# A cross-attention block on Trainium2: another order for the first units, V for two groups of heads at once, and x loaded ahead of the second K chain's weights

## The chip, the cores and the metric

The kernel runs on one core of one Trainium2 chip. The metric is the device time of one execution in microseconds. The core has five engines that run side by side, each through its own list of instructions in program order, and wait for one another by semaphores: TensorE (PE in the profile) multiplies matrices, VectorE (DVE) and ScalarE (ACT) do elementwise work, GpSimd (POOL) does small elementwise work, and SyncE (SP) issues most of the transfers (DMAs). Products land in PSUM and are copied ("evacuated") to SBUF by DVE or ACT.

## What is computed

One transformer block with cross-attention, in float32, for B = 4 batches of 512 tokens of width 512, 16 heads of 32, and an inner width of 2048. The mask, here all ones, is applied too.

```python
x = layer_norm(hidden_states, ln1_w, ln1_b)
q = (x @ q_w + q_b).reshape(B, LQ, H, HD).transpose(0, 2, 1, 3)
k = (encoder_hidden_states @ k_w + k_b).reshape(B, LK, H, HD).transpose(0, 2, 1, 3)
v = (encoder_hidden_states @ v_w + v_b).reshape(B, LK, H, HD).transpose(0, 2, 1, 3)
scores = jnp.einsum('bhqd,bhkd->bhqk', q, k) * scale
scores = jnp.where(mask, scores, mask_value)
out = jnp.einsum('bhqk,bhkd->bhqd', jax.nn.softmax(scores, axis=-1), v)
hidden = out.transpose(0, 2, 1, 3).reshape(B, LQ, D) @ cproj_w + cproj_b + residual
y = layer_norm(hidden, ln2_w, ln2_b)
y = jax.nn.gelu(y @ fc_w + fc_b, approximate=True) @ proj_w + proj_b
return hidden + y
```

## The kernel before

The attention is cut into 16 units w = 0 to 15: four batches, and in each four groups of four heads (128 columns). Unit w belongs to batch w // 4. For each unit three "chains" of products are made: K (`prep_k`, line 235), Q (`prep_q`, line 245) and V (`prep_v`, line 257). K and Q have 512 moving columns and four blocks of the contraction; V computes 128 tokens by 128 columns at a time, four token tiles by four blocks. In the trace each float32 product shows as two passes, so a K chain is 8 matmuls and a V chain 32. ACT evacuates every chain; POOL then adds V's bias (`v_bias`).

A unit has four quarters of 128 query tokens. A quarter is: `scores` (line 279: four products into the single PSUM tile sc; then DVE adds the mask and takes the least value, line 284, and ACT takes the exponential, line 288) and `turn` (line 302: DVE transposes blocks of 32 by 32 into a tile tb). After every second quarter the reciprocal of the sums is made on DVE (line 307), spread by ACT (line 309) and transposed (line 311), and `copies` (line 345) issues 16 DMAs on SP that exchange tb's blocks between partitions, into pT or a part of gt or xe. `attend` (line 362, "av") multiplies the result by V; it comes some quarters later, at places that the table `AT` sets.

The rest of PE's work is laid between the scores by hand: the lists `first[w]` and `later[w]`. Where `first[w]` is a tuple, its parts run after quarter 0, 1, 2 and 3 of the unit. `A(w)` is a unit's K, Q and V chain; `inputs(b)` is batch b's load of x, its first layer norm (three parts), the four transposed tiles "tp" (`ln1_turn`, line 176) and the load of the context (`load_enc`, into eT, which is the first half of xe). A chain's function also issues the next load into the weights that it has just used: K's, Q's and V's weights have two buffers each, and a load waits until the chain that used the buffer two units before is done. The context has one buffer, so batch 1's context may be loaded only when the last K and V chain of batch 0 are done; it is issued by the item that holds V3.

All these transfers go through SP, in program order: a DMA that waits holds back what is behind it, and what is issued runs on one queue. The first layer norm of batch b is normalised on DVE, and two of its four transposed tiles are evacuated there, unless (1, b) is in `BY_ACT`; then ACT does both. The transposed tiles, chains, av and output projections share four PSUM buffers, taken in turn (pool ps_acc).

The middle of the kernel adds the output projection (line 403), the second layer norm and the MLP (lines 469 and 479) between the scores; from about 560 us on the MLPs of the last batches run alone (lines 573 and 613).

Of the kernel before, what the change touches and what calls it, by code (L numbers as in the profile page):

```python
# [45 lines left out]
P = 128  # L46
# [17 lines left out]
IN_XE = (25, 27, 29, 31)  # L64

AT = {u: (u - 5) // 2 for u in (5, 7, 9, 11, 13, 15, 17, 19, 53, 55, 57, 59, 61, 63)}
BY_ACT = ((1, 1),)
MW = 8
WARM = 9
PW = 2 * NT * HG * HD  # L70
# [7 lines left out]
def xattn_block(ctx: ExitStack, tc: tile.TileContext, x, encT, mask, q_w, k_w, v_w, c_w, fc_w, p_w, vecs, rows, out):  # L78
# [3 lines left out]
    def pools(stack, **bufs):  # L82
        return [stack.enter_context(tc.tile_pool(name=n, bufs=k)) for n, k in bufs.items()]

    const, keep, hids, tiles, small = pools(ctx, const=1, keep=1, hids=6, tiles=4, small=4)
    dram = ctx.enter_context(tc.tile_pool(name="dram", bufs=1, space=bass.MemoryType.DRAM))
    ps_acc = ctx.enter_context(tc.tile_pool(name="ps_acc", bufs=4, space=PSUM))

    att = ctx.enter_context(ExitStack())
    one, two, five = pools(att, one=1, two=2, five=5)  # L90
    ps_sc = att.enter_context(tc.tile_pool(name="ps_sc", bufs=1, space=PSUM))
    ctx.enter_context(tc.manual_schedule())

# [34 lines left out]

    def kqv_w(w, i):
        n = 4 * i + 2 + w % 2  # L130
        return ptt[:, n * D : (n + 1) * D].rearrange("p (d f) -> p d f", d=ND)

    S = {}
# [6 lines left out]

    def ln_stat(key, t, src):
        if t == 0:
            S["mv", key] = small.tile([P, NT, 2], F32, tag="mv", name=f"mv{key[0]}_{key[1]}")
        st = small.tile([P, 6], F32, tag="st", name=f"st{key[0]}_{key[1]}_{t}")
        nc.vector.bn_stats(st, src)
        nc.vector.bn_aggr(S["mv", key][:, t, :], st)

    def ln_rs(key):

        ve = small.tile([P, NT], F32, tag="ve", name=f"ve{key[0]}_{key[1]}")  # L150
        nc.gpsimd.tensor_scalar(ve, S["mv", key][:, :, 1], EPS, 1.0, ALU.add, ALU.mult)
        rs = small.tile([P, NT], F32, tag="rs", name=f"rs{key[0]}_{key[1]}")
        nc.gpsimd.tensor_tensor(rs, ve, nhalf, ALU.pow)
        S["rs", key] = rs
        if key in BY_ACT:
            nm = small.tile([P, NT], F32, tag="nm", name=f"nm{key[0]}_{key[1]}")
            nc.gpsimd.tensor_tensor(nm, S["mv", key][:, :, 0], rs, ALU.mult)
            nc.gpsimd.tensor_scalar(nm, nm, -1.0, 0.0, ALU.mult, ALU.add)
            S["nm", key] = nm
# [60 lines left out]
    def load_w(w, queue=None, names=("wk", "wq", "wv")):  # L220

        if w >= NW:
            return
        g = w % NG
        for i, (n, src) in enumerate((("wk", k_w), ("wq", q_w), ("wv", v_w))):
            if n in names:
                S[n, w] = kqv_w(w, i)
                (queue or Q[0]).dma_start(out=S[n, w], in_=src[:, g, :, :])

    def prep_k(w):  # L230
        b, g = divmod(w, NG)
        kT = k_q(w, 0)
        acc = acc_tile(f"acck_{w}")
        for d in range(ND):
            nc.tensor.matmul(acc, S["wk", w][:, d, :], eT[:, d, :], start=(d == 0), stop=(d == ND - 1))  # L235
        load_w(w + 2, names=("wk",))
        nc.scalar.activation(kT, acc, AF.Identity, bias=vec[:, KB + g : KB + g + 1], scale=1.0)
        S["kT", w] = kT
# [10 lines left out]
        S["qT", w] = qT  # L249

    def prep_v(w):
        b = w // NG
        v = five.tile([P, NT, P], F32, tag="v", name=f"v_{w}")
        acc = acc_tile(f"accv_{w}")
        for t in range(NT):
            for d in range(ND):
                nc.tensor.matmul(  # L257
                    acc[:, ts(t, P)], eT[:, d, ts(t, P)], S["wv", w][:, d, :],
                    start=(d == 0), stop=(d == ND - 1),
                )  # L260
        load_w(w + 2, names=("wv",))
        nc.scalar.copy(v, acc.rearrange("p (t f) -> p t f", t=NT))  # L262
        S["v", w] = v
        if w:
            v_bias(w)

    def v_bias(w):
        v, bias = S["v", w], row[:, 2, ts(w % NG, P)]
        nc.gpsimd.tensor_tensor(v, v, bias[:, None, :].broadcast_to([P, NT, P]), ALU.add)  # L269


    def scores(w, qt):
        if qt == 0:
            S["sums", w] = small.tile([P, NT, HG], F32, tag="sums", name=f"sums_{w}")
        qT, kT, sums = S["qT", w], S["kT", w], S["sums", w]
        sc = ps_sc.tile([P, HG, L], F32, tag="sc", name=f"sc_{w}_{qt}")
        for h in range(HG):
            r = slice(h * HD, (h + 1) * HD)
            nc.tensor.matmul(sc[:, h, :], qT[r, ts(qt, P)], kT[r, :], start=True, stop=True)  # L279
        ps = []  # L280
        for h in range(HG):
            s = score_tile()
            mn = small.tile([P, 1], F32, tag="mn", name=f"mn_{w}_{qt}_{h}")
            nc.vector.tensor_tensor_reduce(  # L284
                out=s, in0=sc[:, h, :], in1=S["mb", w // NG], scale=1.0, scalar=FMAX,
                op0=ALU.add, op1=ALU.min, accum_out=mn,
            )
            nc.scalar.activation(s, s, AF.Exp, bias=mn, scale=-1.0, accum_out=sums[:, qt, h : h + 1])  # L288
            ps.append(s)
        S["ps", w, qt] = ps  # L290

    def turn(w, qt):

        half, q = divmod(qt, 2)
        if q == 0:


            S["tb", w, half] = two.tile([P, NI, PW + 2 * HD], F32, tag="tb", name=f"tb_{w}_{half}")
        tb = S["tb", w, half]
        tv = tb[:, :, :PW].rearrange("p j (a t h q) -> p a h t j q", a=2, t=NT, h=HG)  # L300
        for h in range(HG - q):
            nc.vector.transpose(tv[:, q, h], S["ps", w, qt][h])  # L302
        if q == 0:
            return

        rs = small.tile([P, 2, HG], F32, tag="rsum", name=f"rsum_{w}_{half}")
        nc.vector.reciprocal(rs, S["sums", w][:, 2 * half : 2 * half + 2, :])
        rr = one.tile([P, 2, HG, HD], F32, tag="rr", name=f"rr_{w}_{half}")
        nc.scalar.copy(rr, rs[:, :, :, None].broadcast_to([P, 2, HG, HD]))
        nc.vector.transpose(tv[:, q, HG - 1], S["ps", w, qt][HG - 1])  # L310
        nc.vector.transpose(
            tb[:, :, PW:].rearrange("p j (a q) -> p a j q", a=2), rr.rearrange("p a h d -> p (a h d)")
        )
        waiting.append((w, half))
        if w < NW - 1 or half == 0:
            exchange()
# [31 lines left out]
    def attend(w, half):  # L348

        b, g = divmod(w, NG)  # L350
        if g == 0 and half == 0:
            S["oT", b] = one.tile([P, NG, L], F32, tag="oT", name=f"oT_{b}")
        v, pT = S["v", w], S["pT", w, half]
        av = acc_tile(f"av_{w}_{half}")
        o = S["oT", b][:, g, ts(half, 2 * P)]
        shape, kw = "p (a i q) -> p a i q", dict(a=2, i=NI)
        pv = pT[:, :, :PW].rearrange("p i (a t h q) -> p t h a i q", a=2, t=NT, h=HG)
        p = [[pv[:, t, h] for h in range(HG)] for t in range(NT)]
        r = pT[:, :, PW:].rearrange("p i (a q) -> p a i q", a=2)
        for t in range(NT):  # L360
            for h in range(HG):
                nc.tensor.matmul(  # L362
                    av[ts(h, HD), : 2 * P].rearrange(shape, **kw), v[:, t, ts(h, HD)], p[t][h],
                    start=(t == 0), stop=(t == NT - 1),
                )
        o, a = o.rearrange(shape, **kw), av[:, : 2 * P].rearrange(shape, **kw)
        nc.vector.tensor_tensor(o, a, r, ALU.mult)
        if (w, half) in held:
            held.remove((w, half))
        exchange()  # L370
# [386 lines left out]
    make_identity(nc, ident)  # L757
    nc.gpsimd.memset(nhalf, -0.5)
    load_enc(0)
    load_w(0, nc.sync, ("wv",))  # L760
    load_x(0)
    load_w(1, nc.sync, ("wk",))
    load_w(0, nc.sync, ("wq",))

    warm = acc_tile("warm")
    for _ in range(WARM):
# [7 lines left out]
    for part in range(3):  # L774
        ln1(0, part)
    prep_k(0)
    prep_v(0)
    prep_k(1)
    run(turns1(0))
    x1, x2, x3, x4 = inputs(1)  # L780
    run(x1)
# [13 lines left out]
    k5, q5, v5 = A(5)  # L795
    k6, q6, v6 = A(6)
    first[0] = (
        [(CHAIN, lambda: prep_v(1))], [(CHAIN, lambda: prep_q(1)), k2] + x2[:1], [k3, v2] + x2[1:2],
        [(CHAIN, lambda: (prep_v(3), load_enc(1)))]
    )  # L800
    first[1] = [q2] + x2[2:], [q3], [k4], x3[:2]
    first[2] = x3[2:] + [v4], [q4], [k5], [v5]
    first[3] = [q5], [k6], [q6], [v6] + do(lambda: c_bias(0))
    mlp = []
    for p in range(SPLIT):
        mlp += FC(p, 0) + FC(p, 1) + PJ(p, 0) + FC(p, 2) + PJ(p, 1) + FC(p, 3) + PJ(p, 2) + PJ(p, 3)
# [24 lines left out]
    def norm(b, *ts_):  # L831
# [7 lines left out]
    later[4] = c[:1] + x2[:1] + c[1:2] + x2[1:2] + c[2:3] + x2[2:] + c[3:]  # L839
    k, q, v = A(8)  # L840
    first[5] = (
        [k] + stat(0, 0, 1, 2, 3) + rs(0) + x3 + norm(0, 0, 1, 2, 3), [v, q] + t2, some(2) + pb_(0), some(2)
    )
    k, q, v = A(9)
    x1, x2, x3, x4 = inputs(3)
# [2 lines left out]
    first[7] = [k, q] + x2[:1] + some(2) + x2[1:2] + some(3) + [v]  # L848

    k, q, v = A(11)  # L850
    first[8] = h_(1, 0, 1) + x2[2:] + [k, q] + x3[:2] + some(1) + x3[2:] + [v] + h_(1, 2, 3) + x4
    later[8] = cb(1) + C(1)
    k, q, v = A(12)
    first[9] = [q] + some(2) + [k] + some(2) + [v]
# [110 lines left out]
```

## Time and profile before

| | us |
|---|---|
| median of 3 runs | 813.45 |
| lowest, highest | 812.35, 814.26 |
| the profiled execution | 812.55 |
| its span, first to last instruction | 810.8 |
| PE busy, in the span | 793.0 |
| DVE busy | 556.2 |
| ACT busy | 355.6 |
| POOL busy | 98.0 |

PE is the busiest engine by far. Some of its work around the place of the change, by PE's timeline: the passes of K0 begin at 5.35 us, V0's at 9.07, K1's at 12.64, the transposed tiles of x at 16.08, Q0's at 17.83, and the first scores at 22.20. The scores of unit 1 begin at 48.29, those of unit 2 at 77.10 and those of unit 3 at 101.85.

```profile
DVE  3786898986678765767778998736738993368511
...
PEclk9998999999999999999999999999999999999999
DMA  8888998857797867688668799883335330023001
```

These are lines of the page's 40 equal slices (20.3 us each): the tenths in which DVE was busy, the clock that the throttle granted to PE, and the share of the DMA engines' time. DVE and the transfers are near their full share in the first 140 us.

### The profile page before, as it was taken

To read this page: it belongs to the slowest core of one execution; us is meant where nothing else is said; L and a number is where in the kernel's file an instruction comes from. 1 tells how busy PE (TensorE), PEld (TensorE's weight loads), DVE (VectorE), ACT (ScalarE), POOL (GpSimd) and SP (SyncE) were. 2 spreads that over 40 slices of the span, in tenths; PEclk is the share of its full clock that TensorE was granted. 3 is DMA by queue.
4 is the path that set the end of the run, shared out by engine and by line. 5 is a ranking of instruction groups with operands and counts; after the bars stand their busy time and mean duration, and the time that the engine had idled before them with its cause. 6 is when DMAs were issued, how large, how long until landed. Compare 5 with 4: busy or idle time off the path is not lost.

```text
span 810.8 us, 11911 instructions
## 1 busy us (share of the span) xinstructions
PE 793.0 (98%) x4082; PEld 481.7 (59%) x4082; DVE 556.2 (69%) x1279; ACT 355.6 (44%) x779; POOL 98.0 (12%) x110
## 2 busy tenths in 40 slices
PE   9996999989999999999999999999999999999998
PEld 6453545454354554535554334445888888888887
DVE  3786898986678765767778998736738993368511
ACT  2664665358673646547644469700312330023200
POOL 1120003030000021001131000120050021200011
PEclk9998999999999999999999999999999999999999
DMA  8888998857797867688668799883335330023001
GB/s 327 284 206 222 210 240 240 236 141 187 187 247 169 230 171 214 164 209 204 158 150 218 189 270 234 208 247 128 97 111 175 112 116 14 27 79 91 1 14 39
DMA packets 60956, 137.14 MB, mean 169 GB/s; under 512 B 12464, under 2 KB 15664, under 8 KB 60768
## 3 DMA queue, kind: packets, MB, share of 16 engines
q1 hardware_dynamic: 59472, 132.43, 60.8%
q0 software_dynamic: 896, 2.82, 1.1%
q10 hardware_dynamic: 528, 1.14, 0.7%
q8 instruction: 32, 0.52, 0.3%
q14 instruction: 28, 0.23, 0.1%
HBM read 58.22 MB, written 6.82 MB: 80 GB/s over the span
## 4 chain that ended last, share of the span: by engine, by line
PE 86%; DVE 5%; SPq 5%; DMA 2%; issue 1%; ACT 0%; POOL 0%; DVEq 0%; POOLq 0%
PE q L573 15%; PE accf L469 9%; PE accp L479 8%; PE accc L403 7%; PE sc L279 7%; PE av L362 7%; PE acck L235 6%; PE accv L257 6%; PE accq L245 6%; SPq L345 5%; PE q5p L613 2%; PE q3p L613 2%; PE q7p L613 2%; PE q6p L613 2%; PE q1p L613 2%; PE q2p L613 2%
## 5 line engine op out<-in xcount | busy, mean ns | idle before, releaser
L288 ACT ACTIVATE ptt<-ptt,mn 128x512 f32<-128x512 f32 x256 | 181.6, 710 | 134.3 <-DVE mn L284 134.2
L284 DVE CUSTOM_DVE_ANT_0 ptt<-sc,mb 128x512 f32<-128x512 f32 x256 | 161.0, 684 | 46.0 <-PE sc L279 45.8
L302 DVE STREAM_TRANSPOSE tb<-ptt 128x512 f32<-128x512 f32 x224 | 142.0, 683 | 5.1 <-ACT ptt L288 5.1
L469 PE MATMUL accf<-yT,pbt 128*128 128x512 f32 x192 | 87.3, 601 | 0.0
L479 PE MATMUL accp<-pbt,gt 128*128 128x512 f32 x192 | 86.4, 600 | 0.0
L279 PE MATMUL sc<-pbt 32*128 32x512 f32 x512 | 73.0, 640 | 3.3 <-DVE mn L284 2.5
L573 PE MATMUL q<-ys,gt 128*128 128x256 f32 x320 | 75.1, 379 | 0.0
L235 PE MATMUL acck<-xe,ptt 128*128 128x512 f32 x128 | 62.0, 629 | 4.2 <-DMA xe<-encT_dram 4.2
L573 PEld LDWEIGHTS q<-ys,gt 128*128 128x128 f32 x320 | 60.8, 190 | 8.3
L257 PEld LDWEIGHTS accv<-ptt,xe 128*128 128x128 f32 x512 | 58.9, 192 | 10.8 <-issue 5.9
L469 PEld LDWEIGHTS accf<-yT,pbt 128*128 128x128 f32 x192 | 35.0, 190 | 50.2 <-issue 46.2
L479 PEld LDWEIGHTS accp<-pbt,gt 128*128 128x128 f32 x192 | 35.2, 190 | 48.6 <-issue 46.2
L257 PE MATMUL accv<-ptt,xe 128*128 128x128 f32 x512 | 60.7, 277 | 2.1 <-DVE xe L179 1.3
L573 PE MATMUL q<-yT,gt 128*128 128x256 f32 x240 | 58.1, 379 | 0.5 <-DVE gt L501 0.5
L245 PE MATMUL accq<-xe,ptt 128*128 128x512 f32 x128 | 58.3, 598 | 0.0
L403 PE MATMUL accc<-wc,oT 128*128 128x512 f32 x128 | 56.7, 597 | 0.0
L269 POOL TENSOR_TENSOR v<-v,row 128x512 f32<-128x512 f32 x16 | 20.5, 1281 | 286.1 <-ACT v L262 286.1
L577 ACT ACTIVATE ga<-uc,vec 128x256 f32<-128x256 f32 x40 | 20.3, 508 | 75.4 <-DVE uc L551 75.4
L573 PEld LDWEIGHTS q<-yT,gt 128*128 128x128 f32 x240 | 45.5, 190 | 7.4 <-DVE gt L501 0.9
L288 ACT ACTIVATION_READ_ACCUMULATOR ptt<-ptt,mn 128x1 f32 x256 | 47.8, 187 | 0.0
L235 PEld LDWEIGHTS acck<-xe,ptt 128*128 128x128 f32 x128 | 24.5, 200 | 39.2 <-issue 31.5
L362 PE MATMUL av<-pT,v 128*32 128x256 f32 x768 | 46.4, 382 | 0.8 <-DMA pT<-tb 0.8
(121 smaller groups left out, 917.4 us busy)
## 6 DMA issues: line engine op xcount, KB each, us to landing
pT<-tb SPq DMA_DIRECT2D x384, 136.0 KB, 2.4
pbt<-p_w_dram SPq DMA_DIRECT2D x40, 256.0 KB, 3.3
gt<-fc_w_dram SPq DMA_DIRECT2D x40, 256.0 KB, 2.7
gt<-tb SPq DMA_DIRECT2D x64, 136.0 KB, 2.5
xe<-tb SPq DMA_DIRECT2D x56, 136.0 KB, 3.1
pbt<-fc_w_dram SPq DMA_DIRECT2D x24, 256.0 KB, 4.3
ptt<-k_w_dram SPq DMA_DIRECT2D x16, 256.0 KB, 3.6
xe<-encT_dram SPq DMA_DIRECT2D x16, 256.0 KB, 4.5
```

Of the source, the lines that this page charges most:

```text
L235: nc.tensor.matmul(acc, S["wk", w][:, d, :], eT[:, d, :], start=(d == 0), stop=(d == ND - 1))
L245: nc.tensor.matmul(acc, S["wq", w][:, d, :], xT[:, d, :], start=(d == 0), stop=(d == ND - 1))
L257: nc.tensor.matmul(acc[:, ts(t, P)], eT[:, d, ts(t, P)], S["wv", w][:, d, :], start=(d == 0), stop=(d == ND - 1),)
L279: nc.tensor.matmul(sc[:, h, :], qT[r, ts(qt, P)], kT[r, :], start=True, stop=True)
L284: nc.vector.tensor_tensor_reduce(out=s, in0=sc[:, h, :], in1=S["mb", w // NG], scale=1.0, scalar=FMAX, op0=ALU.add, op1=ALU.min, accum_out=mn,
L288: nc.scalar.activation(s, s, AF.Exp, bias=mn, scale=-1.0, accum_out=sums[:, qt, h : h + 1])
L302: nc.vector.transpose(tv[:, q, h], S["ps", w, qt][h])
L362: nc.tensor.matmul(av[ts(h, HD), : 2 * P].rearrange(shape, **kw), v[:, t, ts(h, HD)], p[t][h], start=(t == 0), stop=(t == NT - 1),)
L403: nc.tensor.matmul(acc, S["oT", b][:, g, ts(t, P)], wc[:, g, :], start=(g == 0), stop=(g == NG - 1))
L469: nc.tensor.matmul(acc, S["fcw", b, f][:, d, :], S["yT", b][:, d, :], start=(d == 0), stop=(d == ND - 1))
L479: nc.tensor.matmul(acc, gT[q % 2][:, k, ts(t, P)], S["pw", b, q * FQ + k], start=(k == 0), stop=(k == FQ - 1))
L573: nc.tensor.matmul(o, a[:, k], y[:, k], start=(k == 0), stop=(k == 1))
```

## The change

V is computed for two groups of heads at once. `prep_v(w)` now makes half of the tokens for the 256 columns of units w and w + 1 (w even: token tiles 0 and 1; w odd: tiles 2 and 3), in products of 256 columns; the odd one completes V for both. The weights of a pair are one DMA of 512 KB into the place of the two old buffers, so there is one buffer, and the next pair's load is issued when the odd chain is done. V's tile holds two units, with three buffers instead of five.

At the start, x is loaded before the second K chain's weights, and V's weights after Q's; PE runs K0, K1, V0 instead of K0, V0, K1.

The order of the chains in units 0 to 3 is another. On PE, with sc 0_1 for the scores of unit 0, quarter 1, it was sc 0_0, V1, sc 0_1, Q1, K2, sc 0_2, K3, V2, sc 0_3, V3, sc 1_0, Q2, av, sc 1_1, Q3, sc 1_2, K4, av, sc 1_3, two tp tiles, sc 2_0, two tp tiles, V4, av, sc 2_1, Q4, sc 2_2, K5, av, sc 2_3, V5, sc 3_0. It becomes sc 0_0, V1, sc 0_1, V2, K2, sc 0_2, K3, V3, sc 0_3, Q1, sc 1_0, Q2, av, sc 1_1, K4, sc 1_2, V4, av, sc 1_3, Q3, sc 2_0, two tp tiles, K5, av, sc 2_1, two tp tiles, sc 2_2, V5, av, sc 2_3, Q4, sc 3_0. In unit 3, V6 and Q6 change places. The context's load for batch 1 stands one quarter earlier with V3, and so ahead of the second set of exchange copies on SP.

Batch 2's first layer norm goes to ACT. V8 stands before sc 5_1 instead of behind it, and V11 before the last tp tile of batch 3. Small statistics tiles have two buffers instead of four (pool few).

```diff
-BY_ACT = ((1, 1),)
+BY_ACT = ((1, 1), (1, 2))
...
     def kqv_w(w, i):
         n = 4 * i + 2 + w % 2
+        if i == 2:
+
+            return ptt[:, n * D : (n + 2) * D].rearrange("p (d f) -> p d f", d=ND)
         return ptt[:, n * D : (n + 1) * D].rearrange("p (d f) -> p d f", d=ND)
...
-            if n in names:
+            if n in names and (i < 2 or w % 2 == 0):
                 S[n, w] = kqv_w(w, i)
-                (queue or Q[0]).dma_start(out=S[n, w], in_=src[:, g, :, :])
+                (queue or Q[0]).dma_start(out=S[n, w], in_=src[:, g // 2 if i == 2 else g, :, :])
...
     def prep_v(w):
-        b = w // NG
-        v = five.tile([P, NT, P], F32, tag="v", name=f"v_{w}")
+
+        half, first = w % 2, w - w % 2
+        if half == 0:
+            S["v", first] = S["v", w + 1] = three.tile([P, NT, 2 * P], F32, tag="v", name=f"v_{w}")
+        v = S["v", w]
         acc = acc_tile(f"accv_{w}")
-        for t in range(NT):
+        for t in range(2):
             for d in range(ND):
                 nc.tensor.matmul(
-                    acc[:, ts(t, P)], eT[:, d, ts(t, P)], S["wv", w][:, d, :],
+                    acc[:, ts(t, 2 * P)], eT[:, d, ts(2 * half + t, P)], S["wv", first][:, d, :],
                     start=(d == 0), stop=(d == ND - 1),
                 )
-        load_w(w + 2, names=("wv",))
-        nc.scalar.copy(v, acc.rearrange("p (t f) -> p t f", t=NT))
-        S["v", w] = v
+        if half:
+            load_w(w + 1, names=("wv",))
+        nc.scalar.copy(v[:, ts(half, 2), :], acc.rearrange("p (t f) -> p t f", t=2))
...
-                    av[ts(h, HD), : 2 * P].rearrange(shape, **kw), v[:, t, ts(h, HD)], p[t][h],
+                    av[ts(h, HD), : 2 * P].rearrange(shape, **kw), v[:, t, ts(w % 2 * HG + h, HD)], p[t][h],
...
     load_enc(0)
-    load_w(0, nc.sync, ("wv",))
     load_x(0)
     load_w(1, nc.sync, ("wk",))
     load_w(0, nc.sync, ("wq",))
+    load_w(0, nc.sync, ("wv",))
...
     prep_k(0)
+    prep_k(1)
     prep_v(0)
-    prep_k(1)
     run(turns1(0))
...
     first[0] = (
-        [(CHAIN, lambda: prep_v(1))], [(CHAIN, lambda: prep_q(1)), k2] + x2[:1], [k3, v2] + x2[1:2],
-        [(CHAIN, lambda: (prep_v(3), load_enc(1)))]
+        [(CHAIN, lambda: prep_v(1))], [v2, k2] + x2[:1], [k3, (CHAIN, lambda: (prep_v(3), load_enc(1)))] + x2[1:2],
+        [(CHAIN, lambda: prep_q(1))]
     )
-    first[1] = [q2] + x2[2:], [q3], [k4], x3[:2]
-    first[2] = x3[2:] + [v4], [q4], [k5], [v5]
-    first[3] = [q5], [k6], [q6], [v6] + do(lambda: c_bias(0))
+    first[1] = [q2] + x2[2:], [k4], [v4], [q3]
+    first[2] = x3[:2] + [k5], x3[2:], [v5], [q4]
+    first[3] = [q5], [k6], [v6], [q6] + do(lambda: c_bias(0))
...
-        [k] + stat(0, 0, 1, 2, 3) + rs(0) + x3 + norm(0, 0, 1, 2, 3), [v, q] + t2, some(2) + pb_(0), some(2)
+        [k] + stat(0, 0, 1, 2, 3) + rs(0) + x3 + norm(0, 0, 1, 2, 3) + [v], [q] + t2, some(2) + pb_(0), some(2)
...
-    first[8] = h_(1, 0, 1) + x2[2:] + [k, q] + x3[:2] + some(1) + x3[2:] + [v] + h_(1, 2, 3) + x4
+    first[8] = h_(1, 0, 1) + x2[2:] + [k, q] + x3[:2] + some(1) + x3[2:3] + [v] + x3[3:] + h_(1, 2, 3) + x4
```

## The prediction

> **What bounds the kernel now.** The page first: TensorE (PE) is busy for 793.0 of 810.8 us, so what it loses in waits is nearly all there is to gain, and its waits come second.
>
> ```profile
> PE 793.0 (98%) x4082; PEld 481.7 (59%) x4082; DVE 556.2 (69%) x1279; ACT 355.6 (44%) x779; POOL 98.0 (12%) x110
> ```
>
> ```profile
> engine line waited for: us in total, times, longest us
> PE acck L235 <- DMA xe<-encT_dram: 4.2, 1, 4.2
> PE sc L279 <- DVE mn L284: 2.5, 2, 1.6
> PE tp L176 <- ACT v L262: 2.3, 1, 2.3
> ...
> PE accv L257 <- DVE xe L179: 1.3, 1, 1.3
> ```
>
> Third, PE's timeline over the place of the longest wait: K4, the first chain on batch 1's context, waits 4.25 us and then takes 6.57 us instead of 3.4.
>
> ```profile
> 59.56 1.14 PE L279 MATMUL sc<-pbt 32*128 32x512 f32 x8
> 64.95 6.57 PE L235 MATMUL acck<-xe,ptt 128*128 128x512 f32 x8 [4.25 <-DMA xe<-encT_dram]
> ...
> 77.10 1.14 PE L279 MATMUL sc<-pbt 32*128 32x512 f32 x8 [1.63 <-DVE mn L284]
> ```
>
> Fourth, why. The stage table (PEclk is the third number from the end) has the clock at half after the wait, from 63.98 (0.98 in the row of 63) to 70.78 (0.61 in that of 70); SP's queue shows the context's load behind sixteen exchange copies.
>
> ```profile
> 63.00:64.00 1.00, 0.00 (x0) 0.00 (x0) 1.00 (x5) 1.00 (x3) 0.00 (x0) 0.98 0.95 342
> 64.00:65.00 1.00, 0.05 (x1) 0.08 (x1) 1.00 (x3) 0.96 (x4) 0.00 (x0) 0.50 0.98 281
> ...
> 69.00:70.00 1.00, 1.00 (x2) 0.34 (x1) 0.00 (x0) 0.00 (x0) 0.00 (x0) 0.50 0.78 185
> 70.00:71.00 1.00, 1.00 (x3) 0.34 (x1) 0.00 (x0) 0.00 (x0) 0.00 (x0) 0.61 0.84 212
> 71.00:72.00 1.00, 1.00 (x14) 0.39 (x16) 0.00 (x0) 0.45 (x1) 0.00 (x0) 1.00 0.67 170
> ```
>
> ```profile
> 27.14 0.33 SPq L228 DMA_DIRECT2D ptt<-v_w_dram  x1
> 33.62 11.65 SPq L345 DMA_DIRECT2D pT<-tb  x16
> ...
> 50.03 10.36 SPq L345 DMA_DIRECT2D gt<-tb  x16
> 60.50 0.52 SPq L228 DMA_DIRECT2D ptt<-v_w_dram  x1
> 61.07 1.87 SPq L189 DMA_DIRECT2D xe<-encT_dram  x4
> ```
>
> Below, K4 is the K chain of unit 4, sc 1_2 the scores of unit 1, quarter 2. Steps are counted from start to start on PE's timeline: a chain inside a row of chains 3.43 us, between scores 3.63 (55.93 to 59.56), scores 1.07, av 1.87.
>
> **The change, part by part, with PE walked in its new order.**
>
> *V in 256 columns.* A V chain is 32 passes of 128 columns from 9.07 to 12.64, 3.57 us; afterwards 16 passes of 256. Line 613 runs sixteen such in a row from 585.16 to 588.62, 3.46 us. The saving is 0.12 us (rounded up) x 16 chains = 1.9 us; from below 0, if these operands run differently.
>
> *Context load.* V3 is done before sc 0_3, so the load of encT stands ahead of the second set of copies. By the walk V3 ends at 49.3 and the pieces land by 49.3 + 0.5 (V's own load) + 1.87 + 5.0 (the longest early landing of such a piece) = 56.7; K4 comes at 63.7. Both losses go: 64.95 - 60.63 = 4.32, and K4's 6.49 - 3.43 = 3.06. Two short waits nearby, 77.10 - 75.43 = 1.67 and 80.11 - 79.22 = 0.89, lose their place too. Removed: 9.94 us.
>
> *Start.* K1 follows K0 directly, but its weights become the tenth transfer of the queue, where x's last tile stood: issued at 5.24, landed 6.0 later, 11.2. K0's step ends at 9.07; K1 starts at 11.33 (K4 started 0.14 after its piece landed). Added: 2.26 us. Nothing hides it: DVE's x work ended early anyway, the transposes having waited for PE (16.08). They end at 19.97 instead of 17.83, sc 0_0 starts at 24.35 instead of 22.20.
>
> *One buffer for V's weights.* The pair's weights take both places of the old two, so the next pair's load waits for V1, and V2 stands right behind sc 0_1. Queued behind the SP wait is only what has time (the copies start at 33.6 at the earliest). The walk: V1 to 29.06, sc 0_1 to 30.13. The load is 512 KB behind context, x and c_w loads; the stream up to its end carries the same bytes as the old one up to the load issued at 27.14, which landed 6.9 us on, at 34.05. If the stream does not run dry, V2 starts at 34.2 with K2 queued behind it: 4.07 us added. From below, a load alone in the queue, 3.3 us after issue (0.73 to 4.06 for the first), would give 2.4 us; from above, an x load that leaves the stream dry (its issue now waits for the transposes) adds 0.4.
>
> *The clock after it.* No row shows a 4.1 us idle of PE. The nearest above is 4.25, after which the clock fell 3.3 us into the idle and stayed at half for 6.8 us; the nearest below is 2.28 (at 175), after which the table has 1.00. Ends: 0, and half of the work done at half clock, (70.78 - 64.95) / 2 = 2.9. I take 2.9: the gap is 0.2 from the upper row and 1.8 from the lower. [...]
>
> *Q1 last in unit 0.* sc 1_0 now needs Q1's result at once, and ACT evacuates it behind the reciprocal's copy, which waits for DVE's transposes. Before, sc 0_3 began at 43.45 and ACT was free for the next evacuation at 49.43, 5.98 later; evacuation to scores took 22.20 - 21.46 = 0.74. So sc 1_0 starts 6.72 after sc 0_3 instead of 1.07 + 3.54 = 4.61. Added: 2.12 us.
>
> *Two tp tiles alone between sc 2_1 and sc 2_2.* This is the old pattern of 73.31 to 77.10, 3.79 between scores against 2.12 of PE work: 1.67 us, added again here. Added in all: 2.26 + 4.07 + 2.12 + 1.67 = 10.12.
>
> *Batch 2's normalisation on ACT, V8 earlier.* The 2.28 wait at 175 was for V8's evacuation, behind DVE's long run. V8 now evacuates before sc 5_1, but the fourth tp tile needs Q8's buffer, free after ACT's copy at 176.7 + 0.65. So two transposed tiles no longer wait but one does: 178.48 becomes 177.9, 0.55 us. ACT's four more normalisations (2.9 us) fit its idle 155.4 to 161.3; DVE's relief of two copies goes into the wait for POOL's ve and rs (1.44 at the start), so its exponentials come no earlier.
>
> *V11 before the last tp tile.* V11 takes a buffer evacuated by ACT instead of the one behind DVE: the 1.26 us at 282.5 go; V11's 3.5 us hide the rest. The smaller pool "few" costs nothing by its uses (each buffer's last reader is a unit older).
>
> *Sum.* 9.94 - 10.12 + 1.9 + 0.55 + 1.26 = 3.5 us gained without the clock, 0.6 with it. The profiled execution took 812.55 us (span 810.8 and 1.75 around it), inside the runs' 812.35 to 814.26 and 0.9 below their median; I keep its base: 811.9.
>
> **Rivals.** *B, the clock stays.* 812.55 - 3.5 = 809.0. For it: the idle is shorter than the one seen; against: only by 0.2.
>
> *C, slower: the exchange copies become the bound.* From unit 1 on SP issues two sets of 16 copies a unit; in the walk tb is ready 6.6 us after its second scores (85.74 to 92.35), so a set starts at 92.7 and must land, 2.4 after its last issue, by av 2_0 at 105.8: a set may take 10.7 us. Old sets took 11.65, 10.36, 13.02, 10.83 and 10.04. At 11.65 five sets in a row come 0.95 late each: 4.75 us on top, 816.7. It decides from 10.7 us a set. For it: sets beside loads took 11.65 and 13.02. Against: the later ones did not, and SP has fewer V loads among them.
>
> *D, V's wider passes save nothing*, their loads being hidden already: 811.9 + 1.9 = 813.8. For it, 190 ns of weight load against passes of 112 ns runs hidden before too; against, line 613's row.
>
> **Numbers.** A, the sum with the fallen clock: 0.43; B 0.30; C 0.15; D 0.12. About 0.2% (1.6 us, so 811.8 and 815.1) is what a measurement here can tell from no change. A lies on the lower bound: 0.20 faster, 0.23 the same. B is faster but for 0.01, C slower but for 0.01, D the same but for 0.02; and I move 0.02 from the same to slower for waits not seen. That makes 0.49, 0.33, 0.18. A's own range is 810.7 to 813.3: the 6.8 us at half clock can cover all work or half of it (3.4 or 1.7 lost), the stream can run dry (0.4), a wait of 0.5 can be missing. All cases: 808.2, below B by half of what the V load's lower end would give, to 815.4, between D and C.
>
> **What would show it.** Four PE waits in the first 100 us: on k_w's load near 9.2 (2.1 us), on v_w's near 30 (4.1), scores on ACT near 54 (2.0), scores on DVE near 88 (1.6); none on encT. PEclk at 0.50 from about 33 to 40 decides A against B. V steps of 3.45 refute D. An av wait on pT over 0.5 us is C's mark. At 174 a tp wait of about 2 on Q's evacuation, at 282 none. I am wrong in kind if v_w lands well before 33, if sc 1_0 does not wait, or if a wait appears after unit 3 that was not there.

## The result, and the profile after

The changed kernel takes 823.92 us (median of 822.40 to 825.07), the kernel before 813.31 (812.35 to 814.26) in the same comparison: a ratio of 1.0139, 95% interval 1.0124 to 1.0153. It is 1.4% slower; the forecast was 811.9, with a range of 808.2 to 815.4. The profiled execution took 822.4 us, its span is 9.85 us longer than that of before. Line numbers of the changed kernel are 3 to 6 higher than those of before for the same code.

From its page, the span and the busy times, which answer to the first fence of before. PE has 256 instructions fewer and is busy 3.8 us longer:

```profile
span 820.6 us, 11383 instructions
...
PE 796.8 (97%) x3826; PEld 473.4 (58%) x3826; DVE 554.8 (68%) x1273; ACT 360.0 (44%) x785; POOL 98.7 (12%) x112
```

Its waits (engine, tile and line, what released it, us in total, times, longest). K4's 4.2 us on encT of before have gone; a wait on V's weights and a longer one of a transposed tile are new, as is av's:

```profile
PE accv L263 <- DMA ptt<-v_w_dram: 5.1, 1, 5.1
PE tp L179 <- ACT pbt L251: 3.3, 1, 3.3
PE sc L285 <- ACT pbt L251: 2.7, 2, 1.9
PE sc L285 <- DVE mn L290: 2.5, 2, 1.6
PE av L368 <- issue: 2.0, 2, 1.4
```

Where the 9.85 us came from is read by laying the starts of the same scores side by side; "forecast" is the prediction's terms put into the same stretches, with 0.12 for each V chain:

| stretch, by scores (unit_quarter) | measured | forecast | what it holds |
|---|---|---|---|
| start to 0_0 | +2.87 | +2.15 | first loads, K1's weights |
| 0_0 to 0_2 | +7.24 | +6.87 | V2's weights, fallen clock |
| 0_2 to 1_0 | +1.76 | +1.86 | Q1 |
| 1_0 to 1_1 | +1.65 | 0 | a second fall of the clock |
| 1_1 to 1_3 | -7.16 | -7.38 | encT's wait removed |
| 1_3 to 4_0 | -1.48 | -1.25 | units 1 to 3 |
| 4_0 to 5_0 | +0.60 | -0.12 | av waits 0.65 |
| 5_0 to 6_0 | +4.16 | -0.67 | normalisation, transposed tile, a third fall of the clock |
| 6_0 to 7_0 | +1.30 | -0.12 | av waits for copies |
| 7_0 to 8_1 | -0.12 | -0.12 | |
| 8_1 to 9_0 | -1.69 | -1.38 | V11 earlier |
| 9_0 to the end | +0.72 | -0.48 | -1.02 to +1.17 in seven kernels with the same work there |
| sum | +9.85 | -0.64 | |

The first two waits on PE's timeline (start, length, what, the idle before it and its releaser):

```profile
36.07 5.85 PE L263 MATMUL accv<-ptt,xe 128*128 128x256 f32 x16 [5.14 <-DMA ptt<-v_w_dram]
...
53.44 1.14 PE L285 MATMUL sc<-pbt 32*128 32x512 f32 x8
54.51 3.70 PE L248 MATMUL accq<-xe,ptt 128*128 128x512 f32 x8
60.16 1.39 PE L285 MATMUL sc<-pbt 32*128 32x512 f32 x8 [1.94 <-ACT pbt L251]
61.47 1.22 PE L248 MATMUL accq<-xe,ptt 128*128 128x512 f32 x1
```

and the stage table over both (PEclk is the third number from the end): the clock falls to half at 33.6, in the idle of 5.14, for 6.8 us, and again at 60.9, behind the idle of 1.94, for 3.4 us.

```profile
33.00:34.00 1.00, 0.00 (x0) 0.00 (x0) 1.00 (x5) 1.00 (x5) 0.00 (x0) 0.81 0.87 352
...
40.00:41.00 1.00, 1.00 (x5) 0.82 (x4) 0.00 (x0) 0.00 (x0) 0.00 (x0) 0.78 1.00 231
...
60.00:61.00 1.00, 0.84 (x8) 0.31 (x8) 0.00 (x0) 0.10 (x1) 0.00 (x0) 0.96 0.15 55
61.00:62.00 1.00, 1.00 (x5) 0.50 (x2) 0.41 (x1) 0.00 (x0) 0.00 (x0) 0.50 0.88 196
...
64.00:65.00 1.00, 1.00 (x3) 0.46 (x2) 1.00 (x4) 1.00 (x3) 0.00 (x0) 0.83 0.72 161
```

Unit 5 holds the largest miss. The timeline of VectorE (DVE) and GpSimd (POOL): the four normalisations of batch 0's second layer norm (xn<-h; batch 2's first layer norm is on ACT now) take 3.82 us together, and POOL adds V8's bias and then a row to each of h's four tiles beside them.

```profile
175.55 3.82 DVE L170 TENSOR_SCALAR xn<-h,mv,rs 128x512 f32<-128x512 f32 x4 [1.40 <-POOL rs L156]
179.29 0.68 DVE L290 CUSTOM_DVE_ANT_0 ptt<-sc,mb 128x512 f32<-128x512 f32 x1
...
176.19 1.48 POOL L275 TENSOR_TENSOR v<-v,row 128x512 f32<-128x512 f32 x1 [0.68 <-ACT v L269]
177.64 5.33 POOL L380 TENSOR_TENSOR h<-h,row 128x512 f32<-128x512 f32 x4
```

In the kernel before the same four took half of that, with POOL idle: its adds stood behind V8's bias, and ACT evacuated V8 only at 177.

```profile
170.08 1.91 DVE L167 TENSOR_SCALAR xn<-h,mv,rs 128x512 f32<-128x512 f32 x4
...
177.33 1.29 POOL L269 TENSOR_TENSOR v<-v,row 128x512 f32<-128x512 f32 x1 [7.28 <-ACT v L262]
178.58 2.51 POOL L374 TENSOR_TENSOR h<-h,row 128x512 f32<-128x512 f32 x2
```

The second two of the changed kernel's four take 1.49 us each instead of 0.54. All that hangs on them in turn (masks, exponentials, Q8's evacuation) is late, the fourth transposed tile waits 3.28 us (PE's timeline), and av behind it takes 3.64 instead of 1.93 at a fallen clock (0.50 in the stage table's row):

```profile
184.78 1.11 PE L179 MATMUL tp<-ident,xn 128*128 128x128 f32 x4 [3.28 <-ACT pbt L251]
185.83 3.64 PE L368 MATMUL av<-pT,v 128*32 128x256 f32 x32
```

```profile
185.00:190.00 5.00, 5.00 (x40) 2.40 (x43) 1.45 (x3) 1.18 (x2) 0.00 (x0) 0.50 0.00 0
```

From sc 5_0 to sc 6_0 the kernel is 4.83 us slower than forecast. The slow normalisations are 1.9 of these; the clock is 2.1 (from the fourth tile to sc 6_0 it took 4.62 us, against 2.54 at full clock in the kernel with GpSimd held back, below); and 0.57 came because K8 now waits 0.49 us for batch 2's context, which the forecast did not have.

### The profile page after: what moved, and what is told of

The parts are those of the page before. It is cut to its first block, busy times and chain, and to the rows that moved or that the text cites. A ratio compares the mean times of both kernels' runs of the same rounds, so it can differ in the third digit from the quotient of the medians.

```text
span 820.6 us, 11383 instructions
## 1 busy us (share of the span) xinstructions
PE 796.8 (97%) x3826; PEld 473.4 (58%) x3826; DVE 554.8 (68%) x1273; ACT 360.0 (44%) x785; POOL 98.7 (12%) x112
## 4 chain that ended last, share of the span: by engine, by line
PE 78%; SPq 7%; DMA 6%; DVE 6%; issue 1%; ACT 0%; ACTq 0%; POOL 0%; DVEq 0%
PE q L579 15%; PE accf L475 7%; PE accc L409 7%; PE sc L285 6%; PE av L368 6%; SPq L351 6%; PE accq L248 6%; PE acck L238 6%; PE accv L263 5%; PE accp L485 5%; DVE ptt L290 2%; PE q5p L619 2%; PE q3p L619 2%; PE q7p L619 2%; PE q2p L619 2%; PE q6p L619 2%
## 5 line engine op out<-in xcount | busy, mean ns | idle before, releaser
L263 PE MATMUL accv<-ptt,xe 128*128 128x256 f32 x256 | 60.7, 392 | 5.1 <-DMA ptt<-v_w_dram 5.1
L263 PEld LDWEIGHTS accv<-ptt,xe 128*128 128x128 f32 x256 | 49.3, 196 | 19.8 <-issue 12.1
L368 PE MATMUL av<-pT,v 128*32 128x256 f32 x768 | 48.1, 392 | 3.0 <-issue 2.0
L590 ACT COPY p<-q 128x256 f32<-128x256 f32 x20 | 7.1, 354 | 92.4 <-PE q L579 92.4
```

What stands on the lines that cost most here:

```text
L263: nc.tensor.matmul(acc[:, ts(t, 2 * P)], eT[:, d, ts(2 * half + t, P)], S["wv", first][:, d, :], start=(d == 0), stop=(d == ND - 1),)
L368: nc.tensor.matmul(av[ts(h, HD), : 2 * P].rearrange(shape, **kw), v[:, t, ts(w % 2 * HG + h, HD)], p[t][h], start=(t == 0), stop=(t == NT ...
```

## The experiments

Ratios are to the kernel before on the same chip, with their 95% intervals. One execution of each kernel was profiled; what is said of stretches, waits and landings is read from that one.

**V2's weights early.**

```diff
+        if i == 2 and w == 2:
+            return gt[:, : 2 * D].rearrange("p (d f) -> p d f", d=ND)
...
     load_w(1, nc.sync, ("wv", "wq"))
+    load_w(2, nc.sync, ("wv",))
```

> Edit: the changed kernel, with the V weights of units 2 and 3 loaded at the start into a tile that is unused until unit 0's second exchange, instead of into the place of units 0 and 1's behind V1. Theory (the single place cost a wait and a fallen clock): V2 starts with sc 0_1's end, near 31.0 instead of 36.07, the wait of 5.14 us is gone, the clock does not fall between 33 and 41 (2.24 us), so sc 0_2 starts 7.4 us earlier than in the changed kernel and the end does too: 822.4 - 7.4 = 815.0. Rival (VectorE lived on that pause): the following scores wait for VectorE instead, at least 3 of the 7.4 us come back before unit 2: 818 or more. Both leave Q1's wait (1.9) and unit 5's (3.3) in place.

813.78 us (808.24 to 817.27), ratio 1.0004 (0.9986 to 1.0022). PE's timeline: V2 follows the scores at once.

```profile
34.24 1.14 PE L286 MATMUL sc<-pbt 32*128 32x512 f32 x8
35.31 3.72 PE L264 MATMUL accv<-gt,xe 128*128 128x256 f32 x16
```

From sc 0_0 to sc 0_2 it takes 12.88 us, against 20.21: 7.33 less, as worked out, and nothing came back. In this execution the idle of 1.95 before sc 1_0 was not followed by a fall (1.00 in the rows of 57 to 62 us; 1.65 less again), and its start was 4.44 worse than the changed kernel's: K1 waited 3.28 for its weights, and the clock was at half from 12.6 to 19.5. So the single place for V's weights costs 7.3 us with the clock; the runs spread over 9 us, and K1's wait, 0.28 to 3.28 in the executions of this order, is one thing that varied. The medians are 10.1 us apart; what the 2.8 beyond this stretch come from is not shown.

**GpSimd held back in unit 5.**

```diff
+    def hold():
+        held_mn = few.tile([P, NT], F32, tag="ve", name="hold")
+        nc.gpsimd.tensor_scalar(held_mn[:, :1], S["mn"], 1.0, 0.0, ALU.mult, ALU.add)
...
-... + [v], [q] + t2, some(2) + pb_(0), some(2)
+... + [v], do(hold) + [q] + t2, do(lambda: v_bias(8)) + some(2) + pb_(0), some(2)
```

> Edit: the changed kernel; GpSimd's v bias of unit 8 and its four h adds are held back by one small GpSimd instruction that reads a result of sc 5_1's masks, so that they run behind the second normalisation and not beside it. Theory (VectorE's normalisation is slowed by GpSimd's large adds beside it): all four normalisations near 175 take 0.54 us, sc 5_1's masks start 1.9 us earlier against the normalisation's start, the wait of the fourth transposed tile falls from 3.28 to about 1.4, the clock does not fall (2.9): 822.4 - 1.9 - 2.9 = 817.6. Rival (the two slow normalisations have another cause, such as the exchange copies' traffic or their operands): 1.49 us each stays, and so do the wait and 822.4.

819.71 us, 4.2 below the changed kernel's 823.92; ratio 1.0094 (1.0080 to 1.0108). The timelines of VectorE and GpSimd:

```profile
179.23 1.91 DVE L170 TENSOR_SCALAR xn<-h,mv,rs 128x512 f32<-128x512 f32 x4 [1.40 <-POOL rs L156]
...
183.67 0.19 POOL L275 TENSOR_SCALAR hold<-mn 128x1 f32<-128x1 f32 x1 [4.47 <-DVE mn L294]
183.82 1.30 POOL L279 TENSOR_TENSOR v<-v,row 128x512 f32<-128x512 f32 x1
```

and PE's behind them:

```profile
186.55 0.66 PE L179 MATMUL tp<-ident,xn 128*128 128x128 f32 x4 [1.41 <-ACT pbt L251]
187.23 1.93 PE L373 MATMUL av<-pT,v 128*32 128x256 f32 x32
```

The normalisations take 1.91 again, the tile waits 1.41, the clock stays at 1.00. From sc 5_0 to sc 6_0 it takes 4.58 us less than the changed kernel and 0.41 less than the kernel before, where the forecast had 0.67 less. That is the 1.9 and most of the 2.9 worked out, from when one otherwise idle engine does its adds. In the changed kernel the two normalisations that began during POOL's adds took 1.49 us each and the two others 0.54, and POOL's add of V8's bias took 1.48 beside them and 1.30 here, behind them; by what mechanism is not shown.

**K1's weights ahead of x.** Two lines at the start changed places: `load_w(1, nc.sync, ("wk",))` ahead of `load_x(0)`.

> Edit: the changed kernel with the second K chain's weights loaded ahead of x again, and behind x the rest as it is. Theory (the wait for them was part of what was lost at the start): they land by 9, before K0 ends (10.1 where the clock has risen by then, 11.7 where it has not), and K1 follows K0 without a wait; with this order the wait was 0.28, 1.43, 2.94 and 3.28 us in four profiled executions. sc 0_0 starts at 23.1 or 24.7 by the clock (25.1, 26.2, 26.4 and 29.5 in the four), and the time falls by 1 to 3 us from 823.9: about 822. Rival (x was the need): the transposes at 16.6 to 18.2 wait for x's normalisation, sc 0_0 stays near 26 and the time at 824. A second question: the first load of 256 KB landed at 4.06 in the kernel before and at 5.46 to 5.67 in all five others; this says if that stays so.

820.96 us, 3.0 below the changed kernel; ratio 1.0110 (1.0095 to 1.0125). K1 did not wait, V0 waited 0.85 for its own weights, sc 0_0 started at 24.09, 0.98 earlier than in the changed kernel, and x was not missed. The first load again landed at 5.60. The 0.98 did not last: V2's weights landed at 36.40, V2 waited 6.58 for them, the clock stayed at half for 10.2 us, and at sc 0_2 this execution was 1.29 behind the changed kernel's. Here the earlier start only lengthened that wait. So what loading x first costs by itself is not shown, nor where the 3.0 us between the medians come from.

**Q1 early.**

```diff
-        [(CHAIN, lambda: prep_v(1))], [v2, k2] + x2[:1], [k3, (CHAIN, lambda: (prep_v(3), load_enc(1)))] + x2[1:2],
-        [(CHAIN, lambda: prep_q(1))]
+        [(CHAIN, lambda: prep_v(1))], [(CHAIN, lambda: prep_q(1)), k2] + x2[:1],
+        [k3, v2, (CHAIN, lambda: (prep_v(3), load_enc(1)))] + x2[1:2], [q2]
...
+    first[1] = [q3] + x2[2:], [k4], [v4], [k5]
+    first[2] = x3, [v5], [q4], [q5]
+    first[3] = [k6], [v6], [], [q6] + do(lambda: c_bias(0))
```

> Edit: the changed kernel with another order of units 0 to 3: unit 0 V1 / Q1, K2 / K3, V2, V3 and encT / Q2; unit 1 Q3 / K4 / V4 / K5; unit 2 the four transposed tiles / V5 / Q4 / Q5; unit 3 K6 / V6 / nothing / Q6. Theory (the waits lie in the order alone): V2 comes near 42, behind its weights' landing at 36, Q1 is no longer the last before unit 1, no two tiles stand alone ahead of scores that wait for VectorE: waits of 5.14, 1.94 and 1.63 go, and both falls of the clock (2.24 and 1.65); the empty quarter of unit 3 costs 3.79 - 1.07 - 1.87 = 0.85. 822.4 - 12.6 + 0.85 = 810.6, with encT still ahead of the second set of copies and K4 without a wait. Rival 1 (VectorE sets the pace there): its quarter takes about 5.0 us against 4.5 of a single chain with its scores, and the four tiles put 1.5 us of copies into one quarter; waits of scores for VectorE of 1 to 3 us in units 2 and 3: 812 to 814. Rival 2 (encT behind the copies again): K4 waits 4 us and the clock falls: 817.

820.58 us, ratio 1.0093 (1.0078 to 1.0108): 10 us off the first theory. The three waits and both falls did go, K4 did not wait, but av took over, and from sc 1_3 to sc 4_0 it took 5.4 us more than the changed kernel (PE's timeline):

```profile
84.04 3.39 PE L368 MATMUL av<-pT,v 128*32 128x256 f32 x32 [3.10 <-ACT xe L184]
...
119.25 3.64 PE L368 MATMUL av<-gt,v 128*32 128x256 f32 x32 [3.47 <-DMA ptt<-q_w_dram]
```

Both with a fallen clock (0.50 in the rows of 84 to 86 and of 118 to 123 us): the first waits for a tile that ACT frees, behind its exponentials; the second for its exchange copies, which began at 105.3. Neither rival had named these. Here the quarter of unit 3 that was left without a chain only brought forward the wait for the copies.

**V in 256 columns alone, and pairs alone.** The first has every order of the kernel before. The second is the first with each product split again:

```diff
+            for c in range(2):
                 for d in range(ND):
                     nc.tensor.matmul(
-                        acc[:, ts(t, 2 * P)], ..., S["wv", first][:, d, :],
+                        acc[:, ts(2 * t + c, P)], ..., S["wv", first][:, d, ts(c, P)],
```

> Edit: the changed kernel's V in products of 256 columns, with its weights in a single place, but every order of the kernel before (start, units 0 to 3, 5 and 8) and batch 2's normalisation on VectorE as before. Theory (16 chains at 0.12 us): all waits of the kernel before stay, the V step is 3.45, V2 comes behind Q1, K2 and K3 and does not wait for its weights: 812.55 - 1.9 = 810.6. Rival 1 (the passes' loads were hidden anyway): 812.5. Rival 2 (the single place costs a wait in this order too): a wait of V on its weights over 0.5 us, at 813 or more.

> Edit: the kernel with V alone changed (every order as before), but each product of 256 columns split again into two of 128: what is left of the change is the load of V's weights for two units at once and the pools. It tells apart why that kernel took 814.75 and not 810.6. Theory 1 (the paired loads and the layout cost it): the first load of 256 KB lands at 5.5 again, sc 0_0 starts near 24.7, av waits 1.2 us in unit 7 for copies, the V step is 3.57: 814.75 + 1.9 = 816.6. Theory 2 (the shorter stream of instructions moves TensorE's instruction fetches and cost it): the first load lands at 4.0 as in the two kernels with 128 columns, sc 0_0 near 22.3, no wait in unit 7: 812.7.

814.75 us, 1.0034 (1.0021 to 1.0046), for 256 columns; 813.47, 1.0011 (0.9998 to 1.0025), for pairs with 128. V's step is 3.45 against 3.57, no V waited for its weights for more than 0.16 us, and still the kernel with wide products is the slower of the two by their medians; the intervals touch. Three places differ. One is the first load of 256 KB, issued at 0.73 (DMA issues: KB, us from issue to landing). In the kernel before:

```profile
ptt<-k_w_dram SPq DMA_DIRECT2D x1, 256.0 KB, 3.3
```

in the changed kernel:

```profile
ptt<-k_w_dram SPq DMA_DIRECT2D x1, 256.0 KB, 4.7
```

and in the kernel with pairs and 128 columns:

```profile
ptt<-k_w_dram SPq DMA_DIRECT2D x1, 256.0 KB, 3.4
```

In the 14 profiled executions it landed at 3.95 to 4.41 with products of 128 columns (five) and at 5.46 to 5.67 with 256 (nine), though it is issued before TensorE's first product. Why is open. The second is K4's wait for encT, which stands behind copies: 6.93 and 7.21 us in the two kernels with 256 columns in the order of before, 3.96 to 4.42 in three with 128 (4.05 and a further 1.22 in the fourth). The third is the copies of unit 6's first half (SP's timeline: start, length), in the kernel before:

```profile
217.21 10.02 SPq L345 DMA_DIRECT2D pT<-tb  x16
```

and in the changed kernel:

```profile
226.84 11.47 SPq L351 DMA_DIRECT2D pT<-tb  x16
```

where the DMA queues over that stretch hold an instruction fetch (q8: count, MB, share) and two on another queue. The first is taken to be PE's, as q8 has 32 in the kernel before and 30 in the changed one, whose PE has 256 products and 256 weight loads fewer:

```profile
q8 instruction: 1, 0.02, 0.8%
q14 instruction: 2, 0.02, 0.3%
```

The pairs with 128 columns had neither the late first load nor a wait ahead of unit 7. That is the second theory's picture, and its time within 0.8; that the fetches are the cause is the next kernel's question.

**Fewer instructions in the kernel before.**

```diff
-    for _ in range(WARM):
-        nc.tensor.matmul(warm[:, :P], ident, ident, start=True, stop=True)
+    for _ in range(3):
+        nc.tensor.matmul(warm[:, : 3 * P]..., ident, ident[:, None, :].broadcast_to([P, 3, P]), ...)
```

> Edit: the kernel before, with its nine warming products of 128 columns replaced by three of 384: the same TensorE time, fewer instructions. TensorE's instructions are fetched 16 KB at a time by a DMA of their own; a fetch lay at 216.8 in the kernel before, just ahead of the copies of unit 6's first half (217.2 to 229.0), and 4.5 us into them in all five kernels with V in 256 columns, whose streams are shorter, and there the copies took 13.3 instead of 11.8 us and av waited 1.0 to 1.35 us for them. Theory (the fetch delays a copy, and the set has no slack): some 24 instructions fewer, at 11.6 a us, bring the fetch 2.1 us later, into the set, and av of unit 6's first half waits about 1.2 us, without any other change there: about 814.5. Rival (the wait comes from V's wider products or their larger loads): no wait there, 813.3. It also says if a kernel with V in 128 columns has its first load at 4.06 again.

812.99 us, ratio 1.0007 (0.9997 to 1.0017), and no wait: the theory failed here. The fetch came at 220.5, 4.4 us into the set, about as far in as in the changed kernel, and the set's issues took 0.1 us more. A count over all executions is kinder: of the 210 sets numbered 9 to 23 (the first set is 0), 60 with a fetch of PE inside took 10.21 us from first to last issue in the median (9.54 to 12.08), the 92 without any fetch 9.45 (these leave out the last issue's own 0.6). So sets with a fetch are longer, by 0.8 us in the middle. But six sets without any, all number 14, took 11.3 to 13.9, so other things lengthen a set more, and the one kernel that moved a fetch alone does not show that the fetch does it. The copies of unit 6's first half took 10.57 to 10.88 in six executions with a fetch inside, 9.54 in this one, and 9.43 to 9.98 in the seven without.

**A better order.** V in 256 columns in the order of before, with the edits below; then the same with encT and the weights of units 4 to 7 on GpSimd's queue (`nc.gpsimd` in place of `nc.scalar` and of SP's queue).

```diff
-        [(CHAIN, lambda: (prep_v(3), load_enc(1)))]
+        [(CHAIN, lambda: (prep_v(3), load_enc(1, nc.scalar)))]
...
+    first[1] = [q2] + x2[2:], [q3], [k4], [v4]
+    first[2] = x3[:2] + [k5], x3[2:] + [v5], [q4], [q5]
+    first[3] = [k6], [v6], [], [q6] + do(lambda: c_bias(0))
...
-... + norm(0, 0, 1, 2, 3), [v, q] + t2, ...
+... + norm(0, 0, 1, 2, 3), [v] + A(9)[2:] + [q] + t2, ...
-    first[6] = [k, q] + some(4) + [v] + x1
+    first[6] = [k, q] + some(5) + x1
```

> Edit: V in 256 columns in the order of the kernel before, with encT of batch 1 on ScalarE's DMA queue behind V3's evacuation instead of SP's queue; unit 1 Q2 / Q3 / K4 / V4, unit 2 two transposed tiles and K5 / two and V5 / Q4 / Q5, unit 3 K6 / V6 / nothing / Q6; V9 beside V8 in unit 5, with one more product of the MLP in unit 6; V11 ahead of the last transposed tile. Theory (each wait named so far can be taken away by itself, against the kernel before): encT's wait 4.32 and its clock 3.06, 1.67 and 0.89 of unit 2, 2.28 of unit 5, 1.26 of unit 8, V 1.9, together 15.4; added 0.85 for the empty quarter, 1.2 for the wait on the copies in unit 7 that all kernels with 256 columns had, up to 2.5 at the start: 812.55 - 15.4 + 4.6 = 801.7, and down to 799. Rival (the waits move on): av or V waits for a tile that ScalarE frees late (3.1 and 3.5 us in the kernel with Q1 early), scores wait for VectorE; two of them with a fallen clock: 807 to 810.

> Edit: the reordered kernel with 256 columns, with encT of batch 1 and the weights of units 4 to 7 loaded through GpSimd's queue instead of ScalarE's and SP's. Theory (SP's queue is the pace in units 1 to 3: there its sets began every 12.2 us, 9.6 to 11.5 of copies and 1.25 for two weight loads between them, against 10.87 of TensorE's work in two quarters of one chain, and av waited for them 2.16, 0.27, 0.76 and 4.58 us, the last with a clock that fell): without the loads the sets come every 10.9, the waits shrink to under 1 us together and the clock stays: 809.0 - 7 - 2.4 = 799.6, up to 802. Rival (GpSimd's queue is slow, or its work beside VectorE's transposes slows these): chains wait for weights or scores for VectorE, 806 to 810.

808.97 us, 0.9957 (0.9942 to 0.9972), and 813.86 (808.62 to 819.24), 1.0018 (0.9994 to 1.0041). The waits of units 5 and 8 went for good, those of units 1 to 3 moved to av, 2.16, 0.27, 0.76 and 4.58 us: sc 1_3 came 4.95 us nearer to sc 1_1 than in the kernel before, and sc 4_0 5.05 us further from sc 1_3. GpSimd's queue did not help: one set, beside the loads, took 14.3 us to issue, where the longest had been 11.5, and av waited 6.07 and 3.29. So the loads in SP's queue were not that pace; that the transfers themselves are is not shown, as SP now waited 13.6 us for VectorE's transposes between 44 and 130 us, against 1.8 in the reordered kernel. Moving encT to ScalarE's queue also stopped SP for 7 us, as its waits tell in the reordered kernel:

```profile
SPq L231 <- DMA xe<-encT_dram: 7.2, 2, 7.0
```

By the trace's semaphore numbers, the DMAs of both queues use the same eight semaphores (100 to 107, for 758 DMAs in the kernel before), and there none was issued before the last one with its number had landed (16 ns after it at the earliest); in the reordered kernel K's two loads got those of encT's first two pieces. These landed at 54.43 and 55.07, K's loads were issued at 54.50 and 55.13, and the copies stood behind them.

**The late waits alone, and the width once more.** The kernels with pairs of 128 and with 256 columns, in the order of before but for V9 beside V8 and V11 ahead of the last tile; and the reordered kernel with products of 128 columns.

> Edit: the kernel with V's weights in pairs and products of 128 columns, every order as in the kernel before but two: V9 beside V8 in unit 5 (with one more product of the MLP in unit 6), V11 ahead of the last transposed tile in unit 8. Theory: only the waits of 2.29 and 1.26 us go, 813.5 - 3.5 = 810.0, and nothing else moves. Rival (the copies' sets of unit 6 come late for av, since V9 no longer stands there): a new av wait of 1 us or more in unit 7, 811 or more.

> Edit: as the kernel with the two late waits removed, but V in 256 columns. Theory (as between the two kernels in the order before, 814.75 and 813.47): 1.3 slower than its twin with 128 columns, 811.3. Rival (V's width is worth its 1.9): 808.1.

> Edit: the reordered kernel (809.0) with V's products of 256 columns split into two of 128, nothing else. Theory (the narrow products bring the early first load back, 2.5 us at the start, and lose 16 chains at 0.12): sc 0_0 near 22.7, then the lag grows by 1.9 to the end: 809.0 - 2.5 + 1.9 = 808.4; where av's waits for copies in units 1 to 3 set the pace, V's width counts for nothing there. Rival (the start was chance): sc 0_0 near 25, 810.9.

| order | V in 256 columns | V in pairs, 128 columns |
|---|---|---|
| as before | 814.75, 1.0034 (1.0021 to 1.0046) | 813.47, 1.0011 (0.9998 to 1.0025) |
| two late waits removed | 812.69, 1.0008 (0.9992 to 1.0024) | 810.61, 0.9975 (0.9967 to 0.9984) |
| reordered | 808.97, 0.9957 (0.9942 to 0.9972) | 806.27, 0.9922 (0.9906 to 0.9938) |

The late waits went as worked out (810.0 expected, 810.6 measured, with a new av wait of 0.58). In each order the wide products are slower, by 1.3, 2.1 and 2.7 us between the medians and by 1.9, 2.7 and 2.8 us by the ratios, each on its own chip. Why is open: none of the three places above differs in every pair. sc 0_0 came 2.06, 0.65 and 2.22 us later with the wide products, 0.65 where K0 ran four passes in the row of 7 us, as in the kernel before, in spite of the late load, against two in the other two kernels with wide products; K4's wait differs in the first two pairs, and the copies of unit 6's first half were long in the first alone. In stretches without a wait the wide products save their 0.12 a chain. With the narrow ones the reordered kernel's sc 0_0 came at 22.93 as expected (and at 22.94 in the kernel with wide products and the late waits removed), and the 1.9 us that they should have lost did not show. The last kernel is the fastest of all, 0.8% below the kernel before. Its page:

```profile
span 806.1 us, 11897 instructions
...
PE 791.0 (98%) x4082; PEld 480.7 (60%) x4082; DVE 558.2 (69%) x1279; ACT 361.5 (45%) x783; POOL 96.6 (12%) x110
```

It uses what the pairs made room for, by the program's text: with five buffers of one unit each, as before, V9 in unit 5 would need that of unit 4, which av still reads later.

## Why the prediction was wrong

The forecast was a gain of 0.6 us; it is a loss of 9.85 in the profiled execution, 10.5 us off. Of these, 4.8 lie in unit 5, 1.65 in unit 1, 1.4 in unit 6, and the rest in steps that were off by 1.2 or less each. By its own steps:

- *Context load.* Right: 7.38 worked out, 7.16 measured.
- *Q1 last in unit 0.* Right to the hundredth: sc 1_0 came 6.72 us after sc 0_3. What it set off was not in the sum: an idle of 1.94 and behind it the clock at half from 60.9 to 64.3 us, 1.65.
- *One buffer for V's weights.* Mechanism right, size off: landing at 35.94 instead of 34.05, a wait of 5.14 instead of 4.07. The step's condition was that the stream does not run dry. Loads were outstanding throughout, but in the rows of 26 and 27 us only 158 and 197 GB/s were moved, against 391 and 416 in the kernel before, and x's tile 3 landed 3.3 us behind tile 2. Why the stream slowed is not shown. With its clock this was the largest single cost of the change, 7.3 us by the kernel that takes it away; the forecast had 6.97.
- *The clock after it.* Case A's fall came there (2.2 instead of 2.9), but the step asked only for this one idle. The clock fell three times, with idles of 5.14, 1.94 and 3.28 us. That is the term that was too small: 1.65 in unit 1 and 2.1 in unit 5. The row that the step used, an idle of 2.28 without a fall, spoke against a fall after 1.94; in one of the four executions with this idle it did not come.
- *Start.* 2.15 worked out, 2.87 measured, by another way: the first load came 1.4 later, K0 took 5.36 us, with two passes in each of the rows of 7 and 8 us against four and three in the kernel before (the trace's first record of the full clock begins at 9.72 us, against 5.93), and K1's wait for its weights shrank to 0.28. In other executions of this order it was 1.43 to 3.28. That the sum came near is luck.
- *Batch 2's normalisation on ACT, V8 earlier.* This is the step that failed: 0.55 gained by the forecast (0.67 with V8's chain), 4.16 lost. It took VectorE's four normalisations of batch 0's second layer norm to be as fast as in the kernel before (1.91 us), and moved V8's bias on POOL, with four adds queued behind it, beside them; they took 3.82. The prediction listed what V8's move does on PE and ACT, and not what it issues on POOL. The held-back kernel shows it: 4.58 us back in this stretch, 4.2 in the median, and the stretch is then within 0.3 of the forecast. It also left out K8's wait for batch 2's context, 0.57.
- *V in 256 columns.* The step is 3.45, as forecast; D was refuted in its mechanism. But "The saving is 0.12 us (rounded up) x 16 chains = 1.9 us" took nothing for what 256 products fewer change elsewhere: by the medians of the three pairs of kernels the wide products cost 1.3 to 2.7 us in all, from causes that stay open.
- *V11 before the last tp tile.* Right: with V's saving 1.38 worked out and 1.69 measured.
- *Rival C.* Its mark, av waiting over 0.5 us, appeared before sc 7_0 (1.35) and sc 5_0 (0.65) and in unit 12 (0.71, against 0.30 before), but not in units 1 to 3; V2's wait may have made room there. In the reordered kernel, without that wait, it did come, 4.6 us in one place. It was a rival for a better order than the one it was set against.

The mark "or if a wait appears after unit 3 that was not there" was the one that came true, in units 4, 5 and 6.

## What to carry to other kernels

When a chain is moved, list what it issues on every engine, the idle ones too, and what was queued behind it there: in the kernel before, V8's bias waited 7.28 us in POOL's queue and by accident kept the adds behind it away from VectorE's four normalisations (1.91 us for the four, 3.82 beside the adds). Price an idle of the matrix engine not at its length alone but with the clock behind it (here 1.65 us more with an idle of 1.94, 2.1 with one of 3.28), and count every idle of the new order, not only the longest. A wait that is removed can come back as another one further on, as av's did in units 1 to 3 of the reordered kernel (4.95 us gained, 5.05 lost); look for the next pace before crediting the gain.

## What the runs showed of the hardware

*The clock.* Over the 14 profiled executions, from 8 us on, all 20 idles of PE of 3.0 us and more went with a fall to half, during the idle or up to 1.6 us behind it and for 3.4 us or more; 5 of 12 between 1.87 and 2.94 did, and none of 23 between 1.2 and 1.63 that began at full clock. The shortest idles with a fall were 1.94 or 1.95 us (three times); why these went with one and other idles of up to 2.94 did not is not shown.

*VectorE beside GpSimd.* VectorE's normalisation of 128x512 took 0.54 us alone and 1.48 to 1.51 beside GpSimd's adds of 128x512 (in the four kernels that had them side by side), while its masks, which read the scores from PSUM, took 0.65 to 0.69 either way (in the kernel before and the changed one).

*Fetches.* The queue that the page calls "instruction" (q8) moved 32 transfers of 16 KB (0.52 MB) in the kernel before and 30 in the changed one, one for every 255 of PE's products and weight loads in both. They are taken to be fetches of TensorE's instructions for that, and because one came at 220.5 instead of 216.8 us when nothing but PE's warming products had been made fewer. Sets of copies with such a fetch inside took 0.8 us longer in the median (10.21 against 9.45); that the fetch is the reason is not shown.
